# A Mamba scan whose partitions become 32 channels times 4 states, with the product with C on GpSimd

## The chip, the cores and the metric

The kernel runs on one core of a Trainium2 chip. The core has a tensor engine (TensorE, called PE in the profile, with its weight loads as PEld), a vector engine (VectorE, DVE), a scalar engine (ScalarE, ACT), GpSimd (POOL) and a queue that issues DMAs (SyncE, SP). They run side by side, each takes its own instructions in order, and they wait for each other through semaphores. Operands live in SBUF or in PSUM, where the tensor engine writes; both have 128 partitions. The metric is the time of one execution on the device in microseconds.

## The reference

Four layers follow each other on x of shape [2, 128, 64, 64]: a Mamba block, a convolutional spatial attention, a second spatial attention, and an attention over four scales. The change touches the first. For each of 2 batches and each of 2 Mamba layers, with L = 4096 positions, 128 channels, d = 256 inner channels and N = 16 states, it is cut to what matters:

```python
t = x @ embed_w                                   # residual x is kept
for i in range(2):
    t2 = layernorm(t)
    u, z = split(t2 @ in_w.T)
    u = silu(causal_conv4(u))
    dt, Bm, Cm = split(u @ xproj_w.T)             # 8, 16 and 16 columns
    dt = softplus(dt @ dt_w.T + dt_b)             # [L, 256]
    A = -exp(A_log)                               # [256, 16]
    dA = exp(dt[..., None] * A)
    dBu = (dt * u)[..., None] * Bm[:, :, None, :]
    h_t = dA_t * h_{t-1} + dBu_t                  # scan over L, state [256, 16]
    y_t = sum over n of h_t[:, n] * C_t[n]
    y = (y + u * ssm_D) * silu(z)
    t = t + y @ out_w.T
    t = t + ffn(layernorm(t))                     # 128 -> 512, gelu, -> 128
x = x + t @ outc_w
```

## The kernel before

All data is f32. Channels lie on the partitions and positions along the free dimension, cut into eight chunks of 512 (`NCH`, `CH`). The 256 inner channels are two halves j of 128 (`NJ`). The Mamba stage is a loop over batch b and layer l; in it, per chunk c, four steps:

- `project` (lines 190 to 204): the convolution's taps are folded into the input projection, four matmuls for u (pu) and one for z (pz) for each half, each followed by a Silu on ScalarE. It is called for two chunks at once (`project_pair`), followed by one load of ScalarE's table for exp and ln.
- `prepare` (206 to 230): the matmul pd gives the 40 rows of dt, B and C (tile dbl), pt gives dt before softplus; softplus and dt * u take one pass of small steps on ScalarE and VectorE.
- `scan` (232 to 260): for each of the 16 states n, TensorE copies the row of B (pb, line 237) and of C (pcn, 239) to all 128 partitions; ScalarE makes dA with two Exp (242); VectorE multiplies dt * u with pb (244), runs the recurrence on each half (247) and multiplies h with pcn (249); TensorE adds the product into py through an identity matrix (251). GpSimd only copies the last column of h into the carry (248).
- the chunk's end: u * D + y (254), the product with z on GpSimd (255), the output projection po (259) and the addition to t (260).

Then a layer norm and the FFN follow over the eight chunks. ScalarE keeps the written order (`manual_schedule(engines={ACT})`); the order of the other engines' instructions comes from the framework's scheduler, and each engine then executes its own list strictly in that order. Tiles come from pools with a number of buffers for each tag: a tile whose tag has no free buffer waits until the last reader of the oldest one is done. In the Mamba stage the PSUM pools are mm (2 buffers), bc (4) and yp (one tile of two banks). The weights of the first attention, wq, have a buffer of their own and are loaded at the start.

Of the kernel before, what the change touches and what calls it, by code (L numbers as in the profile page):

```python
# [6 lines left out]
F32 = mybir.dt.float32  # L7
# [26 lines left out]
# Columns of the constants: identity, centring matrix, head selector, statistics selector, ones.  # L34
# [3 lines left out]
# Columns of the per-channel vectors.  # L38
# [15 lines left out]
# Columns of one Mamba layer's weights.  # L54
WL_IN, WL_XP, WL_MO, WL_W1, WL_W2 = 0, 512, 592, 848, 1360
NWL = 1872
# Columns of the small square weights.
# [5 lines left out]
def tile_conv_seq(ctx: ExitStack, tc, x, consts, vecs, wemb, wlay, wconv, wdt, wqkv, wsmall, wms, out):  # L63
# [8 lines left out]
    wbig = ctx.enter_context(tc.tile_pool(name="wbig", bufs=1))  # L72
# [5 lines left out]
    def xv(b, c):  # L78
        """Eight rows of the image, as [P, 8, 64]."""
        return xt[:, b, 1 + c * RPC : 1 + (c + 1) * RPC, 1 : W + 1]  # L80
# [20 lines left out]
    def pick(row, k, m=P):  # L101
        """Weights that copy row `row` of a k-row operand to m output rows."""
        return ident[:k, row : row + 1].to_broadcast([k, m])

    def layer_norm(n, src, centred, dst, g, beta, sp, mm, mmtag, stat, stattag):
        """Normalises n tiles [P, 512] over the partitions. The statistics of tile i are row i."""
# [14 lines left out]
        # One Newton step: r * (1.5 - 0.5 * v * r * r).  # L121
# [11 lines left out]
    # ---------------------------------------------------------------- Mamba and FFN layers  # L133
    with ExitStack() as s, tc.manual_schedule(engines={ACT}):
# [3 lines left out]
        bc = s.enter_context(tc.tile_pool(name="l0bc", bufs=4, space=PSUM))  # L138
        yp = s.enter_context(tc.tile_pool(name="l0y", bufs=1, space=PSUM))

        nc.scalar.preload_act_table_set(EXP_LN_SET)
        wl, wu, wd, am = [], [], [], []
        for l in range(NL):
            w = wp.tile([P, NWL], F32, name=f"wl{l}")
            nc.sync.dma_start(w, wlay[l])
            cw = sp.tile([P, KC, DI], F32, name="cw", tag="da", bufs=2)
# [3 lines left out]
            # The causal convolution's taps, folded into the projection that it follows.  # L150
# [3 lines left out]
            a = wp.tile([P, NJ * DS], F32, name=f"am{l}")  # L154
            nc.scalar.activation(a, vec[:, VEC[f"A_log{l}"] : VEC[f"A_log{l}"] + NJ * DS], AF.Exp)
            nc.vector.tensor_scalar(a, a, -1.0, None, ALU.mult)
# [3 lines left out]
        wq = wbig.tile([P, 3, 9, C], F32, name="wq", tag="wbig")  # L160
        nc.sync.dma_start(wq, wqkv)
        nc.sync.dma_start(ws, wsmall)

        for b in range(B):
            t = sp.tile([P, N], F32, name="t", tag="t")

            def tv(c, t=t):
                return t[:, c * CH : (c + 1) * CH]

            for c in range(NCH):  # L170
                pe = mm.tile([P, CH], F32, name="pe", tag="mm")
                nc.tensor.matmul(pe, lhsT=we[:, 0, :], rhs=xv(b, c), start=True, stop=True)
                nc.scalar.activation(tv(c), pe, AF.Identity, bias=v1("embed_b"))

            for l in range(NL):
# [10 lines left out]
                carry = sp.tile([P, NJ, DS], F32, name="carry", tag="carry", bufs=2)  # L186
                nc.gpsimd.memset(carry, 0.0)
                us, zs, dts, dtus, dbls = {}, {}, {}, {}, {}

                def project(c):  # L190
                    us[c] = sp.tile([P, NJ, CH], F32, name="u", tag="u", bufs=3)
                    zs[c] = sp.tile([P, NJ, CH], F32, name="z", tag="z", bufs=3)
                    for j in range(NJ):
# [10 lines left out]
                        nc.scalar.activation(zs[c][:, j, :], pz, AF.Silu)  # L204

                def prepare(c):
# [4 lines left out]
                    dbl = dbls[c] = sp.tile([NX, CH], F32, name="dbl", tag="dbl", bufs=2)  # L211
                    nc.scalar.copy(dbl, pd)
                    dt = dts[c] = sp.tile([P, NJ, CH], F32, name="dt", tag="dt", bufs=2)
# [3 lines left out]
                    # softplus(v) = max(v, 0) + log1p(e), e = exp(-|v|);  # L217
                    # log1p(e) = ln(w) + (e - (w - 1)) with w the rounded 1 + e.
# [13 lines left out]
                def scan(c):  # L232
                    dt, dtu, dbl = dts.pop(c), dtus.pop(c), dbls.pop(c)
# [408 lines left out]
```

## Time and profile before

| what | us |
|---|---|
| two runs | 8356.37 and 8371.91, median 8364.14 |
| profiled execution, span from first to last instruction | 8356.1, 0.3 below the faster of the two runs |
| busy: PE, DVE, ACT, POOL | 7501.2, 4824.6, 1893.2, 534.4 |
| first matmul of the first attention (line 382) | 3897.2 |
| Mamba stage from 60 to 896 us (first layer's chunks): PE, DVE busy | 704.94, 671.95 of 836 |
| granted TensorE clock, mean of the execution | 0.901 of full speed |

A group of the profile is read so: line, engine, operation, output <- inputs, shapes, number of records, then total busy time and mean time of one in ns, then the engine's idle time ahead of these instructions and what ended it. A row of the timeline has its start, its length, the engine, the line and the operation, merged where equal instructions follow each other, and in brackets the idle time ahead of it. A row of the windows has the stretch and its length, the busy time and number of records of PE, PEld, DVE, ACT and POOL, the granted clock of TensorE, and the DMA share and rate. One f32 matmul of the program appears as two records.

### The profile page before, as it was taken

What the parts mean: (1) busy time and instruction counts of PE and PEld (TensorE: products, weight loads), DVE (VectorE), ACT (ScalarE), POOL (GpSimd) and SP (SyncE); (2) the same over time, 40 slices, a digit from 0 to 9 for tenths busy, and PEclk for the clock granted to TensorE, in tenths of its full rate; (3) what the DMA queues carried; (4) which work ended last, traced back from release to release, by engine and by line L of the source; (5) the groups of instructions that cost most, each with busy time, mean ns of one, the idle gap of its engine ahead of it and who ended that gap; (6) DMA issues with size and microseconds to landing.
All of it is one profiled execution on the core that took longest, in us unless ns stands there. A gap on an engine that the chain in (4) does not pass through costs nothing.

```text
span 8356.1 us, 52802 instructions
## 1 busy us (share of the span) xinstructions
PE 7501.2 (90%) x20720; PEld 3525.3 (42%) x20720; DVE 4824.6 (58%) x6456; ACT 1893.2 (23%) x2323; POOL 534.4 (6%) x634
## 2 busy tenths in 40 slices
PE   8888988889888988889999999999999888888888
PEld 2222322223222322223577567667677533333333
DVE  5788488784787667793366245556566533332333
ACT  2222222223222222221122112222222111111111
POOL 0000000000000000000000000000000021112111
PEclk8888888888888978889999999999999988888888
DMA  1000000000000000000000000000000000000000
GB/s 49 0 0 0 0 0 0 0 0 0 0 0 0 0 0 0 0 0 0 0 1 1 0 12 1 1 1 1 1 1 1 1 2 3 4 3 2 3 3 4
DMA packets 20664, 20.17 MB, mean 2 GB/s; under 512 B 17200, under 2 KB 17344, under 8 KB 20160
## 3 DMA queue, kind: packets, MB, share of 16 engines
q1 hardware_dynamic: 20416, 16.81, 0.7%
q8 instruction: 162, 2.65, 0.1%
q14 instruction: 86, 0.70, 0.0%
HBM read 12.62 MB, written 4.19 MB: 2 GB/s over the span
## 4 chain that ended last, share of the span: by engine, by line
PE 66%; DVE 24%; issue 5%; ACT 2%; POOL 2%; POOLq 0%; DMA 0%; DVEq 0%; SPq 0%; ACTq 0%
DVE h L247 11%; PE po L360 11%; PE pq L343 11%; PE ptt L356 5%; DVE db L244 5%; PE pp L382 4%; PE py L251 4%; PE po L540 3%; PE pw L537 3%; PE pu L196 3%; PE pr L129 3%; DVE db L249 3%; PE pqkv L491 2%; PE pb L237 2%; PE pf L471 2%
## 5 line engine op out<-in xcount | busy, mean ns | idle before, releaser
L251 PE MATMUL py<-db,kc 128*128 128x512 f32 x2048 | 1222.1, 730 | 369.6 <-DVE db L249 368.1
L247 DVE TENSOR_TENSOR_SCAN h<-da,carry,db 128x512 f32<-128x512 f32 x1024 | 1264.2, 1274 | 8.5 <-DVE db L244 1.5
L242 ACT ACTIVATE da<-dt,am 128x512 f32<-128x512 f32 x1024 | 679.6, 713 | 1491.5 <-DVE h L247 1491.5
L343 PE MATMUL pq<-k,q 128*128 128x512 f32 x2048 | 946.1, 593 | 0.0
L360 PE MATMUL po<-pt,vt 128*128 128x256 f32 x4096 | 926.8, 379 | 0.0
L251 PEld LDWEIGHTS py<-db,kc 128*128 128x128 f32 x2048 | 406.8, 219 | 1123.4 <-DVE db L249 677.2
L350 ACT ACTIVATE sc<-sc,nm 128x4096 f32<-128x4096 f32 x128 | 475.0, 3711 | 1594.3 <-DVE nm L348 1594.3
L360 PEld LDWEIGHTS po<-pt,vt 128*128 128x128 f32 x4096 | 758.5, 190 | 92.5
L345 DVE TENSOR_SCALAR_CACHE_REDUCE sc<-pq 128x1024 f32<-128x1024 f32 x512 | 625.8, 1222 | 258.4 <-PE pq L343 257.6
L357 DVE COPY pt<-ptt 128x512 f32<-128x512 f32 x1024 | 672.2, 685 | 40.6 <-PE ptt L356 38.1
L244 DVE TENSOR_TENSOR db<-dtu,pb 128x1024 f32<-128x1024 f32 x512 | 614.2, 1203 | 38.1 <-PE pb L237 38.0
L237 PE MATMUL pb<-dbl,kc 40*128 40x512 f32 x1024 | 613.9, 681 | 12.3 <-DVE db L244 12.3
L249 DVE TENSOR_TENSOR db<-h,pcn 128x1024 f32<-128x1024 f32 x512 | 620.2, 1211 | 7.7 <-PE pcn L239 0.8
L239 PE MATMUL pcn<-dbl,kc 40*128 40x512 f32 x1024 | 574.7, 642 | 51.9 <-DVE db L244 51.2
L356 PEld LDWEIGHTS ptt<-kc,sc 128*128 128x128 f32 x4096 | 478.6, 141 | 243.5 <-DVE pt L357 107.7
L356 PE MATMUL ptt<-kc,sc 128*128 128x128 f32 x4096 | 562.0, 274 | 9.2 <-ACT sc L350 9.2
L343 PEld LDWEIGHTS pq<-k,q 128*128 128x128 f32 x2048 | 357.4, 190 | 298.0 <-issue 210.0
L370 DVE TENSOR_TENSOR on<-po,rb 128x256 f32<-128x256 f32 x64 | 27.2, 424 | 617.3 <-PE po L360 604.8
L517 DVE TENSOR_REDUCE mx<-pst 128x128 f32<-128x512 f32 x16 | 11.1, 692 | 634.9 <-PE pst L513 634.9
L382 PE MATMUL pp<-xt,wq 128*128 128x512 f32 x864 | 373.1, 592 | 0.8 <-DVE xt L298 0.8
L502 POOL TENSOR_TENSOR prod<-qkv,qkv 128x2048 f32<-128x2048 f32 x64 | 286.8, 4503 | 1323.4 <-PE psc L505 1178.9
L248 POOL COPY carry<-h 128x2 f32<-128x2 f32 x512 | 167.6, 327 | 3110.1 <-DVE h L247 3110.1
(149 smaller groups left out, 6320.4 us busy)
## 6 DMA issues: line engine op xcount, KB each, us to landing
xt<-in_x SPq DMA_DIRECT2D x16, 256.0 KB, 5.0
out<-ot SPq DMA_DIRECT2D x16, 256.0 KB, 2.0
wm<-in_wms SPq DMA_DIRECT2D x1, 2304.0 KB, 9.0
wl<-in_wlay SPq DMA_DIRECT2D x2, 936.0 KB, 7.7
wq<-in_wqkv SPq DMA_DIRECT2D x1, 1728.0 KB, 9.4
cw<-in_wconv SPq DMA_DIRECT2D x2, 512.0 KB, 8.2
ws<-in_wsmall SPq DMA_DIRECT2D x1, 768.0 KB, 10.1
kc<-in_consts SPq DMA_DIRECT2D x1, 328.0 KB
```

Source lines behind the costliest of these rows:

```text
L237: nc.tensor.matmul(pb, lhsT=pick(R + n, NX), rhs=dbl, start=True, stop=True)
L242: nc.scalar.activation(da[:, j, :], dt[:, j, :], AF.Exp, scale=a_l[:, j * DS + n : j * DS + n + 1])
L244: nc.vector.tensor_tensor(db, dtu, pb.unsqueeze(1).to_broadcast([P, NJ, CH]), ALU.mult)
L247: nc.vector.tensor_tensor_scan(h[:, j, :], da[:, j, :], db[:, j, :], carry[:, j, n : n + 1], ALU.mult, ALU.add)
L249: nc.vector.tensor_tensor(db, h, pcn.unsqueeze(1).to_broadcast([P, NJ, CH]), ALU.mult)
L251: nc.tensor.matmul(py[:, j, :], lhsT=ident, rhs=db[:, j, :], start=(n == 0), stop=(n == DS - 1))
L343: nc.tensor.matmul(pq[:, i, :], lhsT=q[:, qa : qa + P], rhs=k[:, at : at + CH], start=True, stop=True)
L345: nc.vector.tensor_scalar(dst, pq, 1.0, None, ALU.mult, ALU.max, accum_out=mx[:, c2 : c2 + 1])
L356: nc.tensor.transpose(pt[:, a, :], sc[:, at : at + P], ident)
L357: nc.vector.tensor_copy(pts[c][:, :, it * P : (it + 1) * P], pt)
L360: nc.tensor.matmul(po, lhsT=vt[:, jt, :], rhs=pts[jt // 4][:, jt % 4, :], start=(jt == 0), stop=(jt == N // P - 1))
L382: nc.tensor.matmul(ps, lhsT=wq[:, which, tap, :], rhs=rhs, start=(tap == 0), stop=(tap == 8))
```

## The change

The scan's 128 partitions become 32 channels times 4 states instead of 128 channels of one state. A half of 128 channels is four groups g of 32 channels; in a group, partition 32 q + d holds channel d and state 4 m + q, and the free dimension holds the four m. So a group is one tile h of 128 x 4 x 512.

- B and C no longer go through two matmuls for every state: `spread_bc` makes them once a chunk, eight matmuls (pb) and eight copies on ScalarE into the SBUF tiles bb and cb, in the layout above.
- For each group two matmuls with a selection matrix (`four`) copy 32 channels of dt and of dt * u to four places (pdt, pdu, in PSUM). VectorE multiplies bb with pdu over 128 x 2048. ScalarE makes dA from pdt with four Exp, into PSUM (da, three buffers). VectorE scans four times, in place in h.
- GpSimd multiplies h with cb (128 x 2048), in place of VectorE.
- The sum over the states is taken after the fourth group of a half: sixteen matmuls with 32 output columns (`sel`), each at its own column tile, in the order m, then g.
- `project` is called for one chunk, after the third group of the chunk before, and `prepare` after the fifth, through the function `between`; `spread_bc` of the next chunk comes after the scan. ScalarE loads its exp and ln table after every `project`.
- To make room, t is kept in the image xt itself, the residual x is read again at the end (xr, sixteen loads), u, z and hid have two buffers in place of three, bc two in place of four, and wq is loaded after the Mamba stage's pools are released.

```diff
-        bc = s.enter_context(tc.tile_pool(name="l0bc", bufs=4, space=PSUM))
+        bc = s.enter_context(tc.tile_pool(name="l0bc", bufs=2, space=PSUM))
+        dap = s.enter_context(tc.tile_pool(name="l0da", bufs=3, space=PSUM))
...
+        sel = wp.tile([P, 32], F32, name="sel")
+        nc.vector.tensor_reduce(sel, ident.rearrange("p (q m) -> p m q", q=4), AX.X, ALU.add)
+        fsel = wp.tile([P, 4, 4, 32], F32, name="fsel")
+        for g in range(4):
+            nc.vector.tensor_copy(fsel[:, g], ident[:, 32 * g : 32 * g + 32].unsqueeze(1).to_broadcast([P, 4, 32]))
+        bsel = wp.tile([NX, 2 * DS, 32], F32, name="bsel")
+        nc.vector.tensor_copy(bsel, ident[:NX, R:NX].unsqueeze(2).to_broadcast([NX, 2 * DS, 32]))
+        def four(g):
+            return fsel[:, g].rearrange("p q d -> p (q d)")
+        def rep(at):
+            return bsel[:, at : at + 4].rearrange("p q d -> p (q d)")
...
-                    for n in range(DS):
-                        pb = bc.tile([P, CH], F32, name="pb", tag="bc")
-                        nc.tensor.matmul(pb, lhsT=pick(R + n, NX), rhs=dbl, start=True, stop=True)
-                        pcn = bc.tile([P, CH], F32, name="pcn", tag="bc")
-                        nc.tensor.matmul(pcn, lhsT=pick(R + DS + n, NX), rhs=dbl, start=True, stop=True)
...
-                        nc.vector.tensor_tensor(db, h, pcn.unsqueeze(1).to_broadcast([P, NJ, CH]), ALU.mult)
-                        for j in range(NJ):
-                            nc.tensor.matmul(py[:, j, :], lhsT=ident, rhs=db[:, j, :], start=(n == 0), stop=(n == DS - 1))
...
+                def spread_bc(c):
+                    dbl = bcs.pop(c)
+                    for i, name in enumerate(("bb", "cb")):
+                        o = sp.tile([P, 4, CH], F32, name=name, tag=name)
+                        for m in range(4):
+                            pb = mm.tile([P, CH], F32, name="pb", tag="mm")
+                            nc.tensor.matmul(pb, lhsT=rep(i * DS + 4 * m), rhs=dbl, start=True, stop=True)
+                            nc.scalar.copy(o[:, m, :], pb)
+                        bcs[c, i] = o
...
                     for j in range(NJ):
+                        py = yp.tile([P, CH], F32, name="py", tag="y")
+                        hs = []
+                        for g in range(4):
+                            pdt = bc.tile([P, CH], F32, name="pdt", tag="bc")
+                            nc.tensor.matmul(pdt, lhsT=four(g), rhs=dt[:, j, :], start=True, stop=True)
+                            pdu = bc.tile([P, CH], F32, name="pdu", tag="bc")
+                            nc.tensor.matmul(pdu, lhsT=four(g), rhs=dtu[:, j, :], start=True, stop=True)
+                            h = sp.tile([P, 4, CH], F32, name="h", tag="h", bufs=6)
+                            hs.append(h)
+                            nc.vector.tensor_tensor(h, bb, pdu.unsqueeze(1).to_broadcast([P, 4, CH]), ALU.mult)
+                            for m in range(4):
+                                da = dap.tile([P, CH], F32, name="da", tag="da")
+                                nc.scalar.activation(da, pdt, AF.Exp, scale=a_l[:, j, g, m : m + 1])
+                                nc.vector.tensor_tensor_scan(h[:, m, :], da, h[:, m, :], carry[:, j, g, m : m + 1], ALU.mult, ALU.add)
+                            nc.gpsimd.tensor_copy(carry[:, j, g, :].unsqueeze(2), h[:, :, CH - 1 : CH])
+                            nc.gpsimd.tensor_tensor(h, h, cb, ALU.mult)
+                            between(4 * j + g)
+                        for m in range(4):
+                            for g in range(4):
+                                nc.tensor.matmul(
+                                    py[32 * g : 32 * g + 32, :], lhsT=sel, rhs=hs[g][:, m, :], start=(m == 0), stop=(m == 3),
+                                    tile_position=(0, 32 * g),
+                                )
+                        nc.vector.scalar_tensor_tensor(u[:, j, :], u[:, j, :], v1(f"ssm_D{l}", j), py, ALU.mult, ALU.add)
...
+                project(0)
                 prepare(0)
+                spread_bc(0)
                 for c in range(NCH):
+                    def between(i, c=c):
+                        if c + 1 < NCH and i == 2:
+                            project(c + 1)
+                        if c + 1 < NCH and i == 4:
+                            prepare(c + 1)
+                    scan(c, between)
                     if c + 1 < NCH:
+                        spread_bc(c + 1)
```

In the changed kernel's numbering the lines that the prediction names are: 247 to 254 prepare, 263 and 264 the spread, 275 and 277 pdt and pdu, 280 the product with B, 283 the Exp, 284 the scans, 285 the carry, 286 the product with C, 290 the sums, 294 u, 295 z, 299 po, 300 the addition to t.

## The prediction

> **What bounds the kernel now.** I read the slices of the page first, then its groups, the timeline of one chunk, and the windows.
>
> ```profile
> PE   8888988889888988889999999999999888888888
> DVE  5788488784787667793366245556566533332333
> POOL 0000000000000000000000000000000021112111
> PEclk8888888888888978889999999999999988888888
> ```
>
> The Mamba stage is the first 19 slices (the attention's first projection starts at 3897 us): both PE and DVE are nearly full there, GpSimd is empty, and PE's clock is granted to 0.8.
>
> ```profile
> L251 PE MATMUL py<-db,kc 128*128 128x512 f32 x2048 | 1222.1, 730 | 369.6 <-DVE db L249 368.1
> L247 DVE TENSOR_TENSOR_SCAN h<-da,carry,db 128x512 f32<-128x512 f32 x1024 | 1264.2, 1274 | 8.5 <-DVE db L244 1.5
> L242 ACT ACTIVATE da<-dt,am 128x512 f32<-128x512 f32 x1024 | 679.6, 713 | 1491.5 <-DVE h L247 1491.5
> L244 DVE TENSOR_TENSOR db<-dtu,pb 128x1024 f32<-128x1024 f32 x512 | 614.2, 1203 | 38.1 <-PE pb L237 38.0
> L249 DVE TENSOR_TENSOR db<-h,pcn 128x1024 f32<-128x1024 f32 x512 | 620.2, 1211 | 7.7 <-PE pcn L239 0.8
> L502 POOL TENSOR_TENSOR prod<-qkv,qkv 128x2048 f32<-128x2048 f32 x64 | 286.8, 4503 | 1323.4 <-PE psc L505 1178.9
> ...
> 144.78 1.19 DVE L244 TENSOR_TENSOR db<-dtu,pb 128x1024 f32<-128x1024 f32 x1
> 145.89 1.21 DVE L249 TENSOR_TENSOR db<-h,pcn 128x1024 f32<-128x1024 f32 x1
> 147.02 2.45 DVE L247 TENSOR_TENSOR_SCAN h<-da,carry,db 128x512 f32<-128x512 f32 x2
> 149.39 1.20 DVE L244 TENSOR_TENSOR db<-dtu,pb 128x1024 f32<-128x1024 f32 x1
> ```
>
> Inside a chunk DVE never waits (8.5 us before 1024 scans). A state costs 149.39 - 144.78 = 4.61 us: two products of 1.11 to 1.13 and two scans of 1.185, start to start. So 16 states are 73.8 us. DVE's other work in a chunk is 9.2 us: L223 2 x 0.75, L225 0.69, L226, L227, L229 and L230 1.22 each, L254 2 x 0.74, L260 0.69. The z products (L255) end the chunks: the seven steps between them are 102 us on average in all four layers (first layer 174.66 to 895.19), the first six 107 (174.66 to 819.11), the last 76, since it prepares nothing. So **83 us of a full chunk of 107 is DVE work, 24 us is idle**, at the chunk's ends:
>
> ```profile
> 174.66 2.34 POOL L255 TENSOR_TENSOR z<-z,u 128x1024 f32<-128x1024 f32 x1 [6.49 <-DVE u L254]
> ...
> 177.63 3.78 PE L259 MATMUL po<-z,wl 128*128 128x512 f32 x4
> ...
> 181.45 0.69 DVE L260 TENSOR_TENSOR t<-t,po 128x512 f32<-128x512 f32 x1 [5.81 <-PE po L259]
> ...
> 895.19 2.34 POOL L255 TENSOR_TENSOR z<-z,u 128x1024 f32<-128x1024 f32 x1 [5.20 <-DVE u L254]
> 897.59 1.99 PE L259 MATMUL po<-z,wl 128*128 128x512 f32 x4 [2.27 <-POOL z L255]
> 899.50 5.36 PE L115 MATMUL var<-sq,kc 128*8 128x512 f32 x12
> 899.61 0.69 DVE L260 TENSOR_TENSOR t<-t,po 128x512 f32<-128x512 f32 x1 [3.36 <-PE po L259]
> ```
>
> One f32 matmul of the program is two records. The pair po takes 1.99 us at 897 but 3.78 us at 177: a 512-column matmul is 0.86 us at full clock (L115: 5.36 / 6 = 0.89) and 1.7 to 1.9 at half.
>
> ```profile
> 100.00:175.00 75.00, 70.56 (x126) 23.63 (x124) 70.88 (x63) 18.63 (x27) 4.98 (x16) 0.86 0.00 0
> ```
>
> Even with PE busy 94% of these 75 us (second column) the mean clock is 0.86.
>
> **The change, per chunk.** There are eight groups (two halves j, four g).
>
> *DVE work.* Product L280, 128x2048: the step from 512 (L260, 0.69) to 1024 elements (1.21) is 0.52 per 512, so 2.25, or 2.17 start to start; eight are 17.4. Scans stay 32 x 1.185 = 37.9. They now read da from PSUM, which no row shows; L244 (one PSUM operand, 1203 ns) against L230 (none, 1203 ns) says nothing is lost; the other bound is L223 against L131 (PSUM 0.75, SBUF 0.48): 0.27 a scan, 8.6 a chunk, 240 in all, which I keep for the range. The product with C leaves DVE. With the other 9.2 this is **64.5 us, 18.5 less**. Were DVE all, 32 x 18.5 = 590 us would go.
>
> *GpSimd.* L286 has L502's shape: 4.50 us, plus a carry copy (L248: 0.19). 4.7 in a group of 6.9 us of DVE work: hidden, except after the fourth and eighth group, whose sums wait for it. L502 varies only from 4492 to 4521 ns beside working DVE, so I take 4.5.
>
> *PE.* Removed: 32 pb/pcn and 32 py matmuls. Added: 16 spreads of dt and dtu, 8 of B and C, 32 sums of 32 columns. What matters is the order, which PE keeps: 13 of the 16 sums of a half stand in one block; behind the first block come pt of the next chunk and pdt/pdu of the sixth group; behind the second po, the eight spreads pb, pdt, three pu of the next projection, and pdu.
>
> *Price of a sum.* L115, whose weights are only 8 columns wide, has the full 0.43 us per record, so alone a narrow matmul gains nothing: 0.86. Nothing in this trace shows two column tiles running together. Bounds: 0.22 (four together) and 0.86 (none; 1.7 at half clock). A matmul being two records in order, the second record of one tile may run beside the first of the next tile, which gives one record, **0.43**; I take it, and it lies between the bounds. The Trainium skill, "TensorEngine Tiling (Array Packing)", Overview, gives "Up to 4×" for a dimension up to 32; by it a sum is 0.22 and the time is the first rival's below.
>
> *Clock.* In a group PE has two matmuls, 1.7 us in 6.9, so it comes to each block at half clock. 13 sums at 0.43 are 5.6 at full and 11.2 at half clock; I take 10. The Trainium skill, "TensorE: Matmul & The Clock Gate", Part 1, has the clock fall to half after one idle window of about 3.4 us and return after one busy window, whatever ran before; by it each block would begin at half clock and end at full, 7 to 9 us, and the sum below would be 16 to 48 us lower for each layer.
>
> *Idle DVE, four places.* (a) **Chunk end**, from the last scan: copy and product 4.7 and hand-over 0.2; sums 10; u 0.75 and hand-over 0.2; z 2.35; po 3.5 (z's end to L260 is 4.4 at half clock, 2.1 at full); then eight pb with eight ACT copies through two PSUM buffers, about 1.05 each (copy L212 0.58, matmul 0.86 to 1.7), 8.4; the first exp, queued on ACT behind the copies, 0.9. That is 31 us to the next scan, with 3.6 of DVE work (u, add, product): 27.4 idle. (b) **Middle**, behind the fourth group: 4.9 + 10 + 0.2 until u, with group five (6.9) beside it; 8 idle, then 2 for pt and Abs before dt. (c) **project(c+1)** now stands between two groups' exps on ACT: two table loads of 1.28, four Silu of 0.65 and five matmuls in between, about 9 us; three da buffers (3.6) and a product (2.2) cover most, 4 idle. In the kernel before a pair of projections cost 22 us of idle DVE (181 to 204) every second chunk; that goes. (d) Twice, a group's pdt and pdu stand behind a sum that waits for GpSimd: 4.9 + 0.9 + up to 3.4 against 6.9, 2.6 idle each.
>
> Idle: 27.4 + 10 + 4 + 5.2 = 46.6. **Chunk: 64.5 + 46.6 = 111 against 107: a gain of 18.5 is eaten by 22 of idle time.** The last chunk of a layer loses prepare (7.1), (c) and 2 of (b): 98 against 76. ACT (32 x 0.69 + 8 copies) and PE stay under that.
>
> *Rest.* A layer's first chunk, ahead of the first step, pays a spread (9) and (b), (c), (d) (19) and saves one projection (half of 22): +16 x 4 = 64, taken from the same rows. The residual xr is loaded two at a time, each behind the use before the last (landing 2 to 5 us, 0.75 of work): 8 us twice. wq (9.4 us to land) now waits for the stage's buffers: 0 to 9.4, I take 5. Layer norm through two instead of four PSUM buffers: 0 to 5 a layer, 12 in all. Together +33. The attentions and the last stage are untouched.
>
> **Sum.** Seven steps were 7 x 102.2 = 715 and become 6 x 111 + 98 = 764: +49 x 4 = +196; +64; +33: **+293** on the span of 8356, so 8649. The median of the two runs stands 8 above the span: 8657, given as **8655**.
>
> **Rivals.**
> - *Four sums together* (chance 0.22): blocks of 10 become 4, so (a) loses 6, (b) less, since pt, dt and Ln then stand in it: chunk 101 to 105, last 90, steps 6 x 103 + 90 = 708, -30 + 97: **8430**. For it: the tiles are disjoint columns. Against: every sum reloads its weights (8-column LDWEIGHTS take 0.09 us).
> - *No sums together* (0.30): 13 x 0.86 to 1.72 = 11.2 to 22; at 17 the two places add 14: chunk 125, last 112, steps 862, +588 + 97: **9050**.
> - *Faster* (0.08): sums together **and** the clock stays full, because the block of sums, po, pb, pu is unbroken. Then (a) is 4.9 + 2.8 + 1 + 2.35 + 2.1 + 7 + 0.9 = 21, idle 17, (b) 4, (c) 4, (d) 1: chunk 90, last 78, steps 618, -388 + 97: **8070**. It decides once a block takes under 3.5 us and the clock in the scan stage is above 0.85. Against it: 0.86 already at 94% busy.
> - *GpSimd slows under DVE* (0.05): at 6.9 us or more a product it is the bound, 8 x 7.2 + (a) + (b): chunk 115 or more, 8750 and up.
> - The forecast: 0.35.
>
> A difference under 2% (8197 to 8531) is about what a measurement of this kernel cannot tell from no change. Faster 0.08, within 2% 0.24, slower 0.68. The range leaves out the faster case and the far end of no sums together: 8390 to 9080.
>
> **What would show it.** DVE busy in the stage falls by 590 us while its idle grows; py's spacing in a block is 0.43 at full clock (0.22 and 0.86 for the rivals); from a chunk's last L284 to the next one's first, 31 us; L286 4.5 us; clock about 0.7 up to the attentions; L300 some 111 us apart. Wrong above all would be the price of a sum and the clock under sparse work.

## The result, and the profile after

The changed kernel takes **8606.45 us** (median of 8602.08 and 8610.83) against 8364.14: a ratio of 1.029, 95% interval 1.026 to 1.032. Its profiled execution has a span of 8608.8 us, 252.7 more than the 8356.1 of before; the first projection of the first attention starts at 4150.4 instead of 3897.2, so all of the difference (253.2) lies in the Mamba stage.

The slices of the changed kernel's page, engine by engine and with TensorE's granted clock:

```profile
PE   7666776668666686666999999999999988888888
DVE  4556455563666535555056426656656523332333
POOL 1333123330333303333000000000000021112111
PEclk7777777778777677777999999999999988888888
```

In the stage (now 19 to 20 slices) VectorE has gone from mostly 7 or 8 tenths busy to 4 to 6, GpSimd from nothing to mostly 3, and PE's clock from 0.8 to 0.7. No engine is full any more. The groups of instructions that matter (busy, mean of one, idle time ahead and its releasers):

```profile
L284 DVE TENSOR_TENSOR_SCAN h<-da,carry,h 128x512 f32<-128x512 f32 x1024 | 1233.5, 1264 | 311.0 <-ACT da L283 292.3 <-DVE h L280 0.9
L286 POOL TENSOR_TENSOR h<-h,cb 128x2048 f32<-128x2048 f32 x256 | 1154.5, 4510 | 20.7 <-POOL carry L285 0.2
L290 PE MATMUL py<-h,sel 128*32 128x512 f32 x2048 | 630.1, 906 | 857.6 <-POOL h L286 854.3 <-POOL carry L209 3.3
L280 DVE TENSOR_TENSOR h<-bb,pdu 128x2048 f32<-128x2048 f32 x256 | 583.2, 2278 | 431.4 <-PE pdu L277 281.3 <-ACT bb L264 148.6
```

VectorE's idle time ahead of 1024 scans was 8.5 us and is 311; ahead of the products with B it is 431, of which 281 until pdu arrives. PE in turn stands 854 us at sums that wait for GpSimd. Two full chunks in the windows (length; busy time and records of PE, PEld, DVE, ACT, POOL; clock; DMA):

```profile
301.13:410.14 109.01, 69.88 (x144) 20.07 (x144) 65.36 (x50) 33.81 (x51) 39.91 (x17) 0.73 0.00 0
410.14:523.00 112.86, 75.76 (x144) 22.97 (x144) 65.46 (x50) 33.81 (x51) 39.93 (x18) 0.70 0.00 0
```

A chunk is 65.4 us of VectorE's work and 43.6 or 47.4 of idle time. The end of one chunk in the timeline, the rows of three engines put in order of time:

```profile
506.69 4.81 DVE L284 TENSOR_TENSOR_SCAN h<-da,carry,h 128x512 f32<-128x512 f32 x4
511.82 4.49 POOL L286 TENSOR_TENSOR h<-h,cb 128x2048 f32<-128x2048 f32 x1
516.37 5.76 PE L290 MATMUL py<-h,sel 128*32 128x512 f32 x26 [5.66 <-POOL h L286]
522.17 0.75 DVE L294 SCALAR_TENSOR_TENSOR u<-u,vec,py 128x512 f32<-128x512 f32 x1 [10.68 <-PE py L290]
523.00 2.34 POOL L295 TENSOR_TENSOR z<-z,u 128x1024 f32<-128x1024 f32 x1 [6.68 <-DVE u L294]
525.39 1.98 PE L299 MATMUL po<-z,wl 128*128 128x512 f32 x4 [3.26 <-POOL z L295]
527.31 10.77 PE L263 MATMUL pb<-dbl,bsel 40*128 40x512 f32 x16
531.82 2.29 DVE L280 TENSOR_TENSOR h<-bb,pdu 128x2048 f32<-128x2048 f32 x1 [3.71 <-ACT bb L264]
539.30 4.81 DVE L284 TENSOR_TENSOR_SCAN h<-da,carry,h 128x512 f32<-128x512 f32 x4 [5.20 <-ACT da L283]
```

From the last scan (ends at 511.50) to the next chunk's first (539.30) it is one chain: product, sums, u, z, po, the spreads, an exp; 27.8 us. At the chunk before it was 33.1 (398.43 to 431.49): there po took 3.78 and the spreads 14.02 instead of 1.98 and 10.77.

### The profile page after: what moved, and what is told of

Same layout as the page of the kernel before. It is cut to its first block, busy times and chain, and to the rows that moved or that the text cites. A ratio compares the mean times of both kernels' runs of the same rounds, so it can differ in the third digit from the quotient of the medians.

```text
span 8608.8 us, 51451 instructions
## 1 busy us (share of the span) xinstructions
PE 7031.5 (82%) x20224; PEld 3253.5 (38%) x20224; DVE 4255.5 (49%) x5726; ACT 2046.7 (24%) x2611; POOL 1569.1 (18%) x634
## 3 DMA queue, kind: packets, MB, share of 16 engines
HBM read 16.81 MB, written 4.19 MB: 2 GB/s over the span
## 4 chain that ended last, share of the span: by engine, by line
PE 56%; issue 21%; POOL 16%; DVE 5%; ACT 2%; DMA 0%; POOLq 0%; DVEq 0%; ACTq 0%
POOL h L286 13%; PE po L407 10%; PE pq L390 10%; PE ptt L403 5%; PE pp L429 4%; PE po L587 3%; PE pw L584 3%; PE pr L128 3%; PE py L290 2%; PE pqkv L538 2%; PE ph L327 1%; PE pf L518 1%; PE psc L552 1%; POOL prod L549 1%; PE pf L332 1%
## 5 line engine op out<-in xcount | busy, mean ns | idle before, releaser
L284 DVE TENSOR_TENSOR_SCAN h<-da,carry,h 128x512 f32<-128x512 f32 x1024 | 1233.5, 1264 | 311.0 <-ACT da L283 292.3
L290 PE MATMUL py<-h,sel 128*32 128x512 f32 x2048 | 630.1, 906 | 857.6 <-POOL h L286 854.3
L286 POOL TENSOR_TENSOR h<-h,cb 128x2048 f32<-128x2048 f32 x256 | 1154.5, 4510 | 20.7 <-POOL carry L285 0.2
L283 ACT ACTIVATE da<-pdt,am 128x512 f32<-128x512 f32 x1024 | 649.8, 660 | 1074.1 <-DVE h L284 772.5
L280 DVE TENSOR_TENSOR h<-bb,pdu 128x2048 f32<-128x2048 f32 x256 | 583.2, 2278 | 431.4 <-PE pdu L277 281.3
L290 PEld LDWEIGHTS py<-h,sel 128*32 128x32 f32 x2048 | 107.9, 150 | 1358.6 <-POOL h L286 1098.8
L277 PE MATMUL pdu<-dtu,fsel 128*128 128x512 f32 x512 | 374.7, 824 | 176.4 <-ACT da L283 176.0
L275 PE MATMUL pdt<-dt,fsel 128*128 128x512 f32 x512 | 415.4, 904 | 59.2 <-DVE h L280 59.2
L285 POOL COPY carry<-h 128x4 f32<-128x4 f32 x256 | 47.9, 187 | 2250.6 <-DVE h L284 2250.6
L263 PE MATMUL pb<-dbl,bsel 40*128 40x512 f32 x512 | 395.7, 951 | 12.2 <-ACT bb L264 9.4
```

What stands on the lines that cost most here:

```text
L280: nc.vector.tensor_tensor(h, bb, pdu.unsqueeze(1).to_broadcast([P, 4, CH]), ALU.mult)
L283: nc.scalar.activation(da, pdt, AF.Exp, scale=a_l[:, j, g, m : m + 1])
L284: nc.vector.tensor_tensor_scan(h[:, m, :], da, h[:, m, :], carry[:, j, g, m : m + 1], ALU.mult, ALU.add)
L286: nc.gpsimd.tensor_tensor(h, h, cb, ALU.mult)
L290: nc.tensor.matmul(py[32 * g : 32 * g + 32, :], lhsT=sel, rhs=hs[g][:, m, :], start=(m == 0), stop=(m == 3), tile_position=(0, 32 * g),)
```

## The experiments

All run against the kernel before on the same chip. The seven steps are those between the first layer's eight z products (188.39 to 953.01 in after); the last two columns are of the same stretch.

| run | us | ratio to before, interval | seven steps, us | DVE idle in them | clock |
|---|---|---|---|---|---|
| before | 8364 | 1 | 720.5 | 141 | 0.85 |
| after | 8606 | 1.029 (1.026 to 1.032) | 764.6 | 312 | 0.71 |
| whole_width | 9123 | 1.090 (1.088 to 1.092) | 870.2 | 417 | 0.74 |
| c_on_vector | 8576 | 1.025 (1.023 to 1.026) | 755.0 | 185 | 0.71 |
| last_group_first | 8285 | 0.991 (0.989 to 0.993) | 685.5 | 235 | 0.73 |
| spread_b_early | 8083 | 0.966 (0.964 to 0.967) | 635.0 | 187 | 0.80 |
| sums_late | 7891 | 0.943 (0.941 to 0.944) | 580.4 | 140 | 0.81 |
| pe_fed_two | 8383 | 1.003 (1.002 to 1.004) | 704.1 | 252 | 0.83 |
| pe_fed_four | 8281 | 0.990 (0.989 to 0.992) | 675.5 | 223 | 0.90 |
| po_fed | 8083 | 0.967 (0.965 to 0.968) | 634.4 | 184 | 0.76 |
| end_fed | 8067 | 0.965 (0.963 to 0.966) | 631.4 | 182 | 0.88 |
| clock_at_end | 8263 | 0.987 (0.985 to 0.989) | 679.1 | 229 | 0.77 |
| best | 7864 | 0.940 (0.939 to 0.942) | 576.4 | 119 | 0.72 |
| best_fed | 7767 | 0.929 (0.927 to 0.930) | 556.1 | 99 | 0.83 |

The theory to be tested: the change takes 18 us per chunk off VectorE, and **the serial chain at the chunk's end and waits in PE's queue** give more than that back. The rivals: the price of the sums, GpSimd as the bound, and PE's lower clock.

**Do four column tiles run together?** (whole_width)

```diff
-sel = wp.tile([P, 32], ...)          # one 32-column selector
+sel = wp.tile([P, 4, P], ...)        # zero outside columns 32g to 32g + 31
...
-py[32 * g : 32 * g + 32, :], lhsT=sel, rhs=hs[g][:, m, :], start=(m == 0), stop=(m == 3),
-tile_position=(0, 32 * g),
+py, lhsT=sel[:, g], rhs=hs[g][:, m, :], start=(m == 0 and g == 0), stop=(m == 3 and g == 3),
```

> The sums over states stand in weights of 128 columns, zero outside their own 32, and accumulate over all sixteen products of a group of 128 channels, so one runs after the other over the whole array; the values are the same. (The small weights of the last stage are loaded behind the Mamba stage to make room.) Theory A, that four column tiles run together: the 13 sums in a row, 5.7 us in the trace of after, take 13 times 0.43 to 0.85 us per pass of two, 11 to 22 us by the clock; twice per chunk that is 11 to 33 us more, the chunk step goes from 111 to 122-135 us and the kernel to 8900-9250 us. Theory B, that a sum costs 0.43 us whether in a tile or not, as the prediction took it: the block stays near 10 us or below, the chunk step within 4 us of 111, the kernel within 8550-8720 us.

Measured: 9123 us, inside theory A's range, and a chunk of 126.3 us. The block of 13 sums (26 records) in its timeline:

```profile
515.97 13.44 PE L291 MATMUL py<-h,sel 128*128 128x512 f32 x26 [6.55 <-POOL h L287]
```

13.4 us instead of 5.7, twice per chunk, is 15.4 us, and the step grew by 15.1 ((870.2 - 764.6) / 7). In the trace its records start one after the other, 0.85 us apart while the clock is halved and 0.43 from the sixth on. In after they start in fours, 7 ns apart, the fours 0.85 or 0.43 us apart. So four tiles do run together, and a sum costs 0.22 us at full clock, 0.43 at half. The Trainium skill, "TensorEngine Tiling (Array Packing)", Overview, gives up to 4 times for a dimension of 32 or less; the run agrees: below, in clock_at_end, 16 sums at full clock take 3.64 us, where 32 records one by one at 0.43 would be 13.8.

**Is GpSimd, or its sharing with VectorE, the cost?** (c_on_vector)

```diff
-nc.gpsimd.tensor_tensor(h, h, cb, ALU.mult)
+nc.vector.tensor_tensor(h, h, cb, ALU.mult)
```

> The product with C stands on VectorE instead of GpSimd. On VectorE it needs no more than the 2.28 us of the product with B of the same shape, so VectorE has some 18 us more per chunk, and the two tails behind a last product are 2.2 us shorter each. Theory A, the chain: the chunk step grows by 18 less 4.5, less what VectorE now does in its idle time (at most 5): 9 to 14 us, the kernel 8880-9050 us. Theory B, that GpSimd at 4.5 us per product, or its sharing of the memory port with VectorE, is what costs the time: the step stays at 111 us or falls, the kernel stays within 8350-8650 us.

Measured: 8576 us, outside what theory A gave and inside theory B's range. VectorE has 16.8 us per chunk more to do (82.2 against 65.4), and the time is a little shorter. Groups and a full chunk of this run:

```profile
L286 DVE TENSOR_TENSOR h<-h,cb 128x2048 f32<-128x2048 f32 x256 | 585.0, 2285 | 18.1 <-POOL carry L285 18.1
L280 DVE TENSOR_TENSOR h<-bb,pdu 128x2048 f32<-128x2048 f32 x256 | 580.5, 2268 | 203.7 <-ACT bb L264 155.1 <-PE pdu L277 48.6
...
299.61:407.06 107.45, 73.06 (x144) 20.32 (x144) 82.22 (x58) 34.18 (x51) 3.85 (x9) 0.73 0.00 0
```

585 us of work came back and cost nothing: the wait for pdu fell from 281.3 to 48.6 us, that of the scans for ACT from 292.3 to 200.3. VectorE's own instructions are as long without GpSimd's 4.5 us products beside them as with them (L280 2268 against 2278 ns, scans 1263 against 1264), so sharing is not the cost here. Of theory B the length of GpSimd's product is left, and the next run shows how it costs: by where its result is waited for.

**The wait in PE's queue.** (last_group_first) In the changed kernel's timeline VectorE waits for pdu four times in a chunk; the rows of PE are those ahead of the last one:

```profile
437.42 2.29 DVE L280 TENSOR_TENSOR h<-bb,pdu 128x2048 f32<-128x2048 f32 x1 [1.12 <-PE pdu L277]
445.96 2.29 DVE L280 TENSOR_TENSOR h<-bb,pdu 128x2048 f32<-128x2048 f32 x1 [1.34 <-PE pdu L277]
455.25 2.29 DVE L280 TENSOR_TENSOR h<-bb,pdu 128x2048 f32<-128x2048 f32 x1 [2.09 <-PE pdu L277]
504.30 2.29 DVE L280 TENSOR_TENSOR h<-bb,pdu 128x2048 f32<-128x2048 f32 x1 [3.12 <-PE pdu L277]
...
498.98 1.91 PE L290 MATMUL py<-h,sel 128*32 128x512 f32 x2 [6.73 <-POOL h L286]
500.82 2.08 PE L275 MATMUL pdt<-dt,fsel 128*128 128x512 f32 x2
502.69 1.50 PE L277 MATMUL pdu<-dtu,fsel 128*128 128x512 f32 x2
```

PE stands 6.73 us at one early sum, until GpSimd has its product, and the next group's pdt and pdu, which need nothing of it, stand behind. (The first of the four waits has three pu ahead of it instead. In the chunk before this one there are two waits, 3.31 and 3.53 us, both behind early sums: 6.8 us.)

```diff
-for g in range(4):
+for g in (3, 0, 1, 2):
     nc.tensor.matmul(
         py[32 * g : 32 * g + 32, :], lhsT=sel, rhs=hs[g][:, m, :], ...
```

> Only the order of the sums over states changes: within each of the four steps the group scanned last is summed first, so no sum can start before the fourth product with C is done, and none stands in PE's queue ahead of the next group's pdt and pdu. In after's trace VectorE waits for pdu four times per chunk (1.12, 1.34, 2.09 and 3.12 us, 7.7 in all) while PE stands at such a sum and waits for GpSimd. Theory A, that this wait costs what it shows, and that the product on VectorE won back its 18 us partly there: the step falls by 4 to 8 us, the kernel to 8340-8480 us. Theory B, that the wait only moves (to PE's clock, which falls in the longer pause, or to the exps): within 2 us of 109, 8540-8670 us.

Measured: 8285 us, 55 below the range of theory A; a step of 97.9 instead of 109.2. With no early sum in the queue the same places read, in this run's timeline:

```profile
404.92 2.26 DVE L280 TENSOR_TENSOR h<-bb,pdu 128x2048 f32<-128x2048 f32 x1
...
419.10 2.26 DVE L280 TENSOR_TENSOR h<-bb,pdu 128x2048 f32<-128x2048 f32 x1
464.15 2.26 DVE L280 TENSOR_TENSOR h<-bb,pdu 128x2048 f32<-128x2048 f32 x1
...
476.21 5.57 PE L290 MATMUL py<-h,sel 128*32 128x512 f32 x32 [5.88 <-POOL h L286]
```

These waits, 7.7 us in one chunk and 6.8 in the next, are gone. The block of sums is no longer for having 16 instead of 13 (four together fill eight slots either way). Every chunk now has the shorter of the two ends (27.9 us), 2.5 below their mean. Together that is 9.8 of the 11.3. **An order of four numbers takes back what the change had lost:** 0.9% below the kernel before (interval 0.7 to 1.1%), which is still less than the 2% that count as a difference here.

**The chain at the chunk's end.** (spread_b_early, sums_late)

```diff
 def between(i, c=c):
...
+    if c + 1 < NCH and i == 7:
+        spread_bc(c + 1, (0,))          # B alone
 scan(c, between)
-if c + 1 < NCH:
-    spread_bc(c + 1)
...
 # in scan, behind the first group's scans
+if cb is None:
+    spread_bc(c, (1,))                  # C alone
+    cb = bcs.pop((c, 1))
```

> B of the next chunk is spread before the last block of sums of this one, while the last product with C runs on GpSimd; C is spread after the first group of scans of the next chunk. No work is added or removed. Theory A, that the chain at the chunk's end (product, sums, u, z, po, eight spreads, first exp) is what holds VectorE: the eight spreads (10.8 to 14.0 us) leave the chain, the chunk step falls from 111 to 95-99 us, the kernel to 8130-8280 us, below the time of before. Theory B, that the lower granted clock makes PE's work long wherever it stands, or GpSimd's 4.5 us per group sets the pace: the step falls by less than 5 us and the kernel stays above 8450 us.

```diff
 # in scan: a half's sums and u, and the chunk's z, po and addition, are kept ...
+late.append(lambda j=j, hs=hs: finish(j, hs))
...
+late.append(close)
 # ... and issued behind the second group of the half or chunk that follows
+if g == 1:
+    while late:
+        late.pop(0)()
```

> As the run before (B spread early, C spread after the first group), and also the block of sums, the update of u, and at the chunk's end z, the output projection and the addition are issued behind the second group of what follows, so that VectorE has two groups of scans to do while GpSimd and PE finish. Theory A, the chain: of 111 us about 65 is VectorE's own work; idle time is left at the projection (5), preparation (6-9) and in short waits for the first exps (some 8), so the chunk step is 85-90 us and the kernel 7850-8050 us. Theory B, that GpSimd (40 us per chunk) or PE at a low clock becomes the bound as soon as VectorE is fed: the step stays above 95 us and the kernel above 8150 us.

Measured: 8083 us, 47 below the range of theory A, and 7891 us, inside it. Moving the spreads is worth 18.5 us a step (109.2 to 90.7), moving the sums and the tail 7.8 more (to 82.9). In after the eight spreads and ACT's copies were 10.8 to 14 us of the chain; the step gains more than that, because VectorE now has work beside the rest of the chain. Here is the same place in spread_b_early, where a product with B and a scan are done before the last sums end, and three scans run beside the tail:

```profile
448.64 2.29 DVE L281 TENSOR_TENSOR h<-bb,pdu 128x2048 f32<-128x2048 f32 x1 [0.99 <-ACT bb L265]
451.04 1.28 DVE L285 TENSOR_TENSOR_SCAN h<-da,carry,h 128x512 f32<-128x512 f32 x1
458.48 0.75 DVE L298 SCALAR_TENSOR_TENSOR u<-u,vec,py 128x512 f32<-128x512 f32 x1 [6.17 <-PE py L294]
459.15 3.62 DVE L285 TENSOR_TENSOR_SCAN h<-da,carry,h 128x512 f32<-128x512 f32 x3
```

No instruction was taken out: the same work in another order is 6 and 8% faster than after.

**Is it the clock?** (pe_fed_two, pe_fed_four, po_fed, end_fed, clock_at_end) The first two add two or four products behind each pdu:

```diff
 nc.tensor.matmul(pdu, lhsT=four(g), rhs=dtu[:, j, :], start=True, stop=True)
+for _ in range(4):                      # 2 in pe_fed_two
+    nc.tensor.matmul(py, lhsT=four(g), rhs=dt[:, j, :], start=True, stop=True)
```

> After each pdu two matrix products of 128 by 512 more are run into the bank of py, which the sums overwrite afterwards; nothing reads them. They only keep PE busy between the groups. Theory A, that the lower clock (0.71 in the stage, 0.85 before) lengthens the chain at the chunk's end: at a full clock the eight spreads would take about 7 us instead of 10.8 to 14.0 and a block of sums 3.4 instead of 5.7, so up to 10 us of 109 could go; with two products per group the clock rises part of the way, the step falls by 2 to 6 us, the kernel to 8420-8560 us. Theory B, that the clock is a sign of the idle PE and costs nothing, or that the added products stand in the way of the next pdt: the step stays or grows, 8600-8800 us.

> The same with four added products after each pdu, 3.4 us at full clock and 6.9 at half in a group of about 8 to 9 us. Theory A: the clock rises further than with two, and the time is at or below that of the run with two, 8380-8560 us, unless the added products delay the next group's pdt, where the gain is lost again. Theory B: slower than the run with two by at least 60 us.

Measured: 8383 and 8281 us, theory A and even below its ranges, and the clock rose to 0.83 and 0.90. But the traces show another reason: the added products write py, so no sum can start ahead of a half's last pdu, which is the change of last_group_first by another way. That run has the clock at 0.73 and takes 8285. **Against it, a mean clock of 0.90, with the products that it takes, brings next to nothing.** The block of sums and the spreads in pe_fed_four:

```profile
471.74 5.32 PE L292 MATMUL py<-h,sel 128*32 128x512 f32 x26 [2.76 <-POOL h L288]
482.23 10.06 PE L263 MATMUL pb<-dbl,bsel 40*128 40x512 f32 x16
```

They are nearly as slow as with the low mean clock (5.57 and 10.94 in last_group_first): PE waits for GpSimd right ahead of the block. In the trace the block's records start 0.43 us apart for three fours and 0.85 after that: the clock falls some 1.2 us after the block has begun. The Trainium skill, "TensorE: Matmul & The Clock Gate", Part 1, has the clock follow a free-running window of some 3.4 us. The traces here agree: the changes of the granted clock lie whole multiples of 3.41 us apart.

The next two were meant to put the added products into the waits of the chain: three into po's bank while z is multiplied, and ten into py's behind the fourth pdu of a half.

```diff
 # po_fed, on last_group_first
 po = mm.tile([P, CH], F32, name="po", tag="mm")
+for _ in range(3):
+    nc.tensor.matmul(po, lhsT=four(0), rhs=dt[:, 0, :], start=True, stop=True)
 # end_fed: also, behind pdu
+for _ in range(10 if g == 3 else 0):
+    nc.tensor.matmul(py, lhsT=four(g), rhs=dt[:, j, :], start=True, stop=True)
```

> On last_group_first (8285 us): three matrix products more into the bank of po, run while GpSimd multiplies z (PE idle for 3.4 us there), overwritten by the projection that follows. The run pe_fed_four raised the mean clock of the stage from 0.73 to 0.90 and was as fast as last_group_first, which shares its order of sums, so the mean clock as such is worth nothing; its eight spreads still took 10.1 us, against 10.9. Theory A, that the clock counts only where PE is on the chain, at the chunk's end, and is lost there because PE idles just before: with PE busy in that gap the spreads fall from 10.9 to 7-9 us, the step by 2 to 4 us, the kernel to 8150-8230 us. Theory B, that the clock is worth nothing there either: 8270-8310 us.

> The run po_fed with ten more products into the bank of py behind the fourth pdu of each half, run while PE waits for the last product with C (some 6 us idle before each block of sums). Theory A: a block of 16 sums falls from 5.5 us to 3.4-4, twice per chunk, and the spreads to about 7 us: the step falls 5 to 8 us below last_group_first's 97.9 (seven steps in 685.5), the kernel to 8020-8130 us. Theory B: as po_fed or slower, because the added products run longer than the wait that they fill.

Measured: 8083 us, even below the range of theory A, and 8067, inside it. In po_fed the spreads are at full clock (1.12 us for one, 2.92 for three), but the added products (L298) do not run while z is multiplied, and five of the spreads have moved. The added products and the end of the chunk on PE in po_fed:

```profile
421.40 2.74 PE L298 MATMUL po<-dt,fsel 128*128 128x512 f32 x6
...
449.00 1.12 PE L263 MATMUL pb<-dbl,bsel 40*128 40x512 f32 x2 [0.68 <-ACT bb L264]
453.02 5.69 PE L290 MATMUL py<-h,sel 128*32 128x512 f32 x32 [2.90 <-POOL h L286]
458.65 1.12 PE L263 MATMUL pb<-dbl,bsel 40*128 40x512 f32 x2
460.44 1.12 PE L263 MATMUL pb<-dbl,bsel 40*128 40x512 f32 x2 [0.68 <-ACT bb L264]
462.11 1.98 PE L301 MATMUL po<-z,wl 128*128 128x512 f32 x4 [0.54 <-POOL z L295]
464.02 2.92 PE L263 MATMUL pb<-dbl,bsel 40*128 40x512 f32 x6
```

The added products read dt, which is ready early, so the framework's scheduler put them into the middle of the chunk, and with that the order of the rest changed: three spreads now stand ahead of the sums (the other two start at 424.07 and 447.20) and two more ahead of po. That is what spread_b_early does, and its time (8083) is the same, though it has the old order of the sums. In end_fed, too, the ten added products run in the middle of the chunk; its mean clock is 0.88, and its block of sums still takes 5.98 us. So a last run made the added products wait for what is ready only there:

```diff
 # on last_group_first, ahead of each block of sums
+for i in range(4):
+    nc.tensor.matmul(py, lhsT=four(0), rhs=hs[2][:, i % 4, :], start=True, stop=True)
 # ahead of po
+for _ in range(3):
+    nc.tensor.matmul(po, lhsT=four(0), rhs=u[:, 1, :], start=True, stop=True)
```

> On last_group_first (8285 us), with its order of sums and spreads. In po_fed and end_fed the added products did not run where they were meant to: PE took them in the middle of the chunk, and four of the eight spreads moved ahead of po, so neither run tells what the clock at the chain is worth. Here the added products read what becomes ready only there: four read the third group's product, so they run just before each block of sums, and three read the new u, so they run while GpSimd multiplies z. Nothing reads their results. Theory A, that the clock lost in PE's wait right before makes the block (5.5 us) and the spreads (10.9) long: the spreads fall to 7-8.5 us, the block to 4-5, the step from 97.9 to 92-95, the kernel to 8100-8200 us. Theory B, that the clock at these places is worth nothing, or that the added products cost what they bring: 8250-8330 us.

Measured: 8263 us, theory B. Its chunk's end on PE, and one wait of VectorE further on in the chunk before:

```profile
465.19 5.97 PE L289 MATMUL py<-h,fsel 128*128 128x512 f32 x8 [5.59 <-POOL h L286]
472.81 3.64 PE L292 MATMUL py<-h,sel 128*32 128x512 f32 x32
477.40 2.84 PE L300 MATMUL po<-u,fsel 128*128 128x512 f32 x6 [0.95 <-DVE u L296]
480.07 1.88 PE L303 MATMUL po<-z,wl 128*128 128x512 f32 x4
481.88 9.45 PE L263 MATMUL pb<-dbl,bsel 40*128 40x512 f32 x16
...
399.77 2.29 DVE L280 TENSOR_TENSOR h<-bb,pdu 128x2048 f32<-128x2048 f32 x1 [1.37 <-PE pdu L277]
```

The block is at full clock now, 3.64 instead of 5.57, and the spreads are 1.5 shorter; the chunk's end falls from 27.9 to 25.2 us (467.40 to 492.56). But a full chunk stays at 99.0: a pdu comes 1.37 us late behind slower pu, and the first exps of the projected group 5.17 instead of 4.38. As far as this run raised the clock at the chain, that is worth about 2.7 us a chunk (some 86 us in 32 chunks, 1% of the kernel), and keeping it there cost nearly as much.

The run did not raise it for the spreads, and after's windows show why feeding PE ahead of them did not do it. The first holds po, the eight spreads and pdt of one chunk, the second the last four spreads and pdt of the next:

```profile
412.54:432.06 19.52, 19.52 (x22) 7.02 (x23) 3.55 (x3) 5.85 (x11) 0.00 (x0) 0.50 0.00 0
530.95:538.01 7.06, 7.06 (x10) 2.36 (x9) 2.29 (x1) 2.34 (x4) 0.00 (x0) 0.50 0.01 2
```

PE is busy without a break, and the clock is 0.50. Seven runs have the eight spreads in one block (after, whole_width, c_on_vector, last_group_first, both pe_fed and clock_at_end), without a break in all chunks but a layer's first. It rose in none of these 196 blocks: 54 are at half clock throughout, and in 142, all 28 of clock_at_end among them, it falls inside the block. So a busy PE does not by itself hold the clock: a block of spreads lets it fall. These matmuls read 40 rows where po and pu read 128; whether that is the reason, no run separates.

**A faster version.** (best, best_fed) best is sums_late with the order 3, 0, 1, 2 and `prepare` cut in two, its pd and dbl issued a group earlier (i == 3, the rest at i == 4). best_fed adds products to it:

```diff
 py = yp.tile([P, CH], F32, name="py", tag="y")
+for _ in range(4):
+    nc.tensor.matmul(py, lhsT=four(0), rhs=dt[:, j, :], start=True, stop=True)
...
 po = mm.tile([P, CH], F32, name="po", tag="mm")
+for _ in range(3):
+    nc.tensor.matmul(po, lhsT=four(0), rhs=dt[:, 0, :], start=True, stop=True)
```

> The run sums_late (7891 us) with two more moves: the group scanned last is summed first, as in the run above, and the preparation of the next chunk is cut in two, so that the small projection to 40 rows and its copy are issued a group ahead of what reads them. In the trace of sums_late VectorE waits some 3 us for pdu behind a sum, and 4.4 us for the first exp of the preparation, per chunk. Theory A, that these are waits on VectorE's path: the step goes from 82.9 (seven steps in 580 us) to 76-80 us, the kernel to 7680-7820 us. Theory B, that they are hidden or replaced: 7850-7920 us.

> The run best (7864 us, clock in the stage 0.72) with four added products ahead of each block of sums and three ahead of the projection po. In best the chain at the chunk's end is gone and VectorE is idle for some 17 us per chunk, 12 of them behind PE (pdu 4.96 and 1.09, po 2.73, bb 3.66). Theory A, that PE at half clock is what holds pdu, po and bb back: the idle time falls by 3 to 5 us, the kernel to 7700-7800 us. Theory B, that the added products, standing in the same queue, cost what they bring: 7840-7920 us.

Measured: 7864 and 7767 us. best missed theory A's range and lies in theory B's. The wait for the preparation's first exp went, but the instruction behind it (w from e, L252; L249 with 0.69 us in sums_late) now fills 4.19:

```profile
471.83 4.53 POOL L316 TENSOR_TENSOR h<-h,cb 128x2048 f32<-128x2048 f32 x1
472.71 4.19 DVE L252 TENSOR_SCALAR w<-e 128x1024 f32<-128x1024 f32 x1
```

It starts while GpSimd multiplies h with cb, and ends some 0.55 us after that product. So it is in the 28 chunks in which the two meet, in best and in best_fed alike; in the four others, and in every other run, where they never meet, it takes 0.69. Here, then, VectorE is held up beside GpSimd, 3.5 us a chunk or some 98 us in best; without them its time, by that estimate 7766, would lie in theory A's range. Beyond that, po ran at half clock (3.78 us, VectorE waiting 2.73), and a pdu came behind 20 records of sums and two spreads (4.96). best_fed gets most of that back; here the three added products run right ahead of z's product (426.42 to 428.77), and po's rows are at full clock:

```profile
423.98 2.84 PE L293 MATMUL po<-dt,fsel 128*128 128x512 f32 x6
428.83 1.98 PE L296 MATMUL po<-z,wl 128*128 128x512 f32 x4 [1.15 <-POOL z L290]
...
430.85 0.69 DVE L297 TENSOR_TENSOR xt<-xt,po 128x512 f32<-128x512 f32 x1 [0.94 <-PE po L296]
```

The waits for po, pdu and the next pdu fell from 2.73, 4.96 and 1.09 us to 0.94, 4.29 and 0.24: 3.3 of the 3.4 by which a chunk shortened (85.3 to 81.9). The other four products changed the order on PE too, so what of this is the clock and what the order stays open. At 7767 us it is 7.1% faster than before (interval 7.0 to 7.3%) and 9.8% faster than after.

## Why the prediction was right, and where it was not

The forecast was 8655 (8390 to 9080) and slower; measured 8606. The sum's parts, in the profiled executions:

| term | predicted | measured |
|---|---|---|
| DVE work less, whole stage | 590 | 574 (2835.6 to 2261.6) |
| seven steps, four layers | +196 | +171 (3032.8 against 2861.7) |
| first chunks (measured with what lies between the layers) | +64 | +65 |
| rest (predicted with 12 for the layer norms; measured at the stage's end) | +33 | +17 |
| full chunk | 111 | 112.9 and 109.0 in turn |
| (a) chunk end, last scan to first | 31 | 27.8 and 33.1, mean 30.4 |
| (b) middle, idle | 10 | 4.9 (3.50 + 1.02 + 0.34) and 5.7 |
| (c) project, idle | 4 | 5.0 and 5.9 |
| (d) idle behind sums and pu | 5.2 | 7.7 and 6.8 |

- **DVE work and GpSimd's price: right.** The product with B takes 2278 ns (predicted 2250), GpSimd's product 4510 (4500), and scans that read PSUM 1264 against 1274 before: the bound of 0.27 more per scan, kept for the range, is ruled out.
- **The step that failed is the price of a sum.** It was put at 0.43 us at full clock, two tiles together at most, because a sum's two records stand in order; the records came in fours, a sum is 0.22, and a block of 13 takes 5.7 to 6.5 us and not 10. That is the condition of the first rival, to which 0.22 of chance was given. By the prediction's own working the time should then have been 8430.
- **It came out at 8606 because other terms were too small.** In (a) the sums gave some 4 back, and the eight spreads, sized 8.4 with the copies, took 10.8 to 14.0, half or all of them at half clock. In (d) the early sums held up three pdu in one chunk and two in the next, with 7.7 and 6.8 us together with the wait behind pu. The errors in (b), 4.3 to 5.1 too much, and in (c) and (d), 3.5 too little, partly cancel too. So the total's closeness is in part luck; the idle time per chunk, 46.6 predicted, is 43.6 and 47.4.
- **The rival "no sums together"** has its own kernel now: 9123 us measured in whole_width, 9050 predicted; its price was right, its condition not met.
- **The rival "faster"** made the clock decide. The runs speak against it without settling it: a mean of 0.90 instead of 0.73 brought next to nothing with the sums equally late, and clock_at_end, with a block at full clock, kept next to nothing. Its condition, a full clock through sums, po and spreads, was met in no run with the spreads in one block. What made the change a gain was the order on PE and at the chunk's end.
- **GpSimd as the bound: no.** It is busy 40 us of 111. Yet its 4.5 us of latency, standing in PE's queue and in the chain, cost as much as the work that it took from VectorE (16.8 us a chunk in c_on_vector).
- **Clock:** predicted about 0.7 in the stage, measured 0.73; right, but this mean explains little. The blocks of sums begin at half clock and end at full, as the rule cited in the prediction has it. The spreads do not follow that rule: 14.02 us of them without a break stay at half.

## What to carry to other kernels

Work taken off the bounding engine is a gain only as far as something else stands ready for that engine at that moment; cost an offload with the latency that it puts in front of whatever waits in the same queues, here PE's. Before a chain is made cheaper, see what of it can be issued earlier or later: moving the spreads out of it was worth 18 us of a 109 us chunk, keeping PE's clock up at the chain, as far as a run did, under 3. When an experiment adds work, look in its trace where the added work really ran, since the scheduler may place it elsewhere and change the order of all the rest. And when an instruction moves, compare its own length before and after: in best one grew from 0.69 to 4.19 us beside GpSimd's product, which no idle time shows.

## What the runs showed of the hardware

- f32 matmuls with 32-column weights on four column tiles start 7 ns apart and take the time of one: 16 sums in 3.64 us at full clock (clock_at_end), against 0.43 us for every record in whole_width, where 128-column weights make them run one by one.
- VectorE's products with B and scans, which read one operand from SBUF and one from PSUM, are as long with GpSimd's 4.5 us products about as without (2278 against 2268 ns, 1264 against 1263). The instruction w from e, which reads and writes SBUF alone, takes 4.19 us instead of 0.69 when it starts during such a product, 28 times of 28 in best.
- A scan that reads one operand from PSUM takes 1264 ns, one that reads all from SBUF 1274.
- The granted clock fell to half 1.2 us after a block of sums had begun, following a wait of 2.8 us (pe_fed_four), and rose 3.2 to 5.8 us after the start of the blocks of sums that began at half in after. In 196 unbroken blocks of eight spreads (seven runs) it never rose. The mean of the stage, 0.73 or 0.90, did not tell the clock of the blocks on the chain.
